# A graph layer on one core: 32 gathers taken from the input in the head, halved head products, constants written early, and columns fetched by ScalarE in two of five groups

## The chip, the core and the metric

The kernel runs on one core of a Trainium2 chip. A core has TensorE (PE in the profile, with its weight loads as PEld), VectorE (DVE), ScalarE (ACT), GpSimd (POOL) and SyncE (SP, which here only issues transfers); each works through its own instructions in their order. They share SBUF, 128 partitions of memory on the chip; matrix products end in PSUM, which DVE and ACT read. Transfers are done by 16 DMA engines, whichever engine issued them. The metric is the device time of one execution in microseconds.

## The reference

One message-passing layer over 12,500 nodes of 64 features and 412,500 edges, sorted by receiver, with 32 features each:

```python
h = jnp.maximum(_layernorm(x, axis=-1), 0.0)
msg_in = jnp.concatenate([h[src], h[dst], edge_attr_32], axis=-1)
messages = silu(msg_in @ W1 + b1) @ W2 + b2
att = jax.nn.softmax(silu(msg_in @ Wa1 + ba1) @ Wa2 + ba2, axis=0)   # over all edges
aggregated = jax.ops.segment_sum(messages * att, dst, num_segments=12500)
out = x + silu(jnp.concatenate([h, aggregated], -1) @ Wu1 + bu1) @ Wu2 + bu2
```

## The kernel before

**Tiling.** Nodes are padded to 98 blocks of 128 (NB = 98, NP = 12,544). Edges come in 403 groups (NG) of 1,024: K = 8 tiles of 128 edges. W1 and Wa1 stand side by side as 128 columns (C), so an edge has 128 sums before its activation: a sender's part, a receiver's part and an edge's part.

**Head** (`gnn_kernel`). Eight chunks of blocks (8, 14 five times, 12, 8) are loaded, normalized and turned (`squares`, `totals`, `deviation`, `normal`, `transpose`); the turned h stays in SBUF as `hT`, two nodes to a column of 128 rows. `senders` (L259-274) multiplies `hT` by the senders' half of the weights, one product of 128 rows by 256 columns for two blocks (L270), ACT copies the result out of PSUM (L272), and SP writes it as the table `ts_d`. Then `windows` computes each edge's offset from its group's first receiver, and the loop at L302-311 makes the receivers' table `tr_d` (L306 on PE, L308 on DVE, written from ACT's queue at L310). `hT_d` (L313) is a copy of `hT` that only `general` reads, the path for inputs that the main path can't take; it isn't run here.

**Main path** (`one_pass`). Constants, the loop's fixed buffers `acts` and `wins`, and the product W2 x Wu1 (`w2u`) are written at its start (L420-470). Per group g, in the order in which the engines get it:

- `begin(g)`: DVE adds what POOL gathered to the products (L573, and L575 for a column tile), ACT takes tanh (L576).
- pieces of `sum_up` for a group some five back: `out_of` copies its sums out of PSUM (L652, ACT), `put` adds them to the running sums (L671/L675/L678, DVE), `project` multiplies by `w2u` (L657), `by_node` makes the weights by receiver (L640, DVE) and sums over edges on PE (L646).
- `burst(g, 0)`: ACT fetches columns for a chosen group ahead, below.
- `load(g + 2)`: POOL gathers eight times 128 rows of `ts_d` by sender (L533) into one of the seven `gs` buffers of the pool `gather`; SP loads edges and receivers for four groups at a time (L544, L547) and two windows of `tr_d` (L554, three buffers); DVE makes the 0/1 matrix `eo` (L558); PE multiplies it with the window, which adds the receivers' and the edges' part (L562).
- `end(g)`: four DVE passes for message and logit (L586-L597), after every fourth group the maximum (`top`, with the exponentials in `weigh`, L627/L630 on ACT).
- `burst(g, 1)`: more columns.

POOL's gathers wait for nothing but the table, a free `gs` buffer and the eighth gather before. DVE, PE and ACT keep the written order (`pin`).

**Chosen groups.** In every third group from 8 to 390 (g % 3 = 1; 127 groups) the eighth tile isn't gathered. ACT copies, for each of its 128 edges, one column of `hT` (L504), whose number it first loads into a register (L500); a burst of 12 to 24 columns stands in each half of an iteration, six for a chosen group. `numbers` loads the sender indices, `places` computes column and parity on DVE (L487-L493, six operations), L567 zeroes the half that belongs to the other node, and PE multiplies by `stack` (L568), both halves of the senders' weights.

Of the kernel before, what the change touches and what calls it, by code (L numbers as in the profile page):

```python
# [53 lines left out]
P = 128  # L54
# [14 lines left out]
B = 4  # L69
NQ = 4  # L70
# [3 lines left out]
EVERY = 3  # L74
PHASE = 1
SLOTS = (((0, 24), (24, 24)), ((48, 24), (72, 12)), ((84, 24), (108, 20)))
# [7 lines left out]
PARTS = [("pair", 4 * C), ("we", C), ("bias", C), ("wu2h", 2 * D), ("wa2", U), ("bu2", D), ("w_bu", U),  # L84
         ("w2b", U), ("wu1a", U), ("wu2", D), ("ba2", 1), ("w_bup", 2 * U), ("bu1", 1)]
# [5 lines left out]
def gnn_kernel(ctx: ExitStack, tc: tile.TileContext, n_edges, x, src, src_row, dst, dst_row, first, edge,  # L91
# [14 lines left out]
    hT_d = dram.tile([2 * D, NB // 2, P], F32, name="hT_d")  # L106
# [19 lines left out]
    w_bu = part["w_bu"][:D + 1]  # L126
# [25 lines left out]
    nc.vector.memset(zero, 0.0)  # L152

# [8 lines left out]
    gather = ctx.enter_context(tc.tile_pool(name="gather", bufs=7))  # L162


    with tc.tile_pool(name="node1", bufs=1) as node1, \
            tc.tile_pool(name="node", bufs=2) as node, \
            tc.tile_pool(name="node_ps", bufs=2, space=PSUM) as node_ps:
        x_v = x.rearrange("(p b) d -> p b d", b=NB)

# [10 lines left out]
        nc.sync.dma_start(src_full, src)  # L180
# [11 lines left out]
        def windows():  # L192
# [6 lines left out]
            pin(nc.vector.tensor_tensor(dloc[:, T - K:], dloc[:, T - K:], real, ALU.mult))  # L199
            for h in range(2):  # L200
                pin(nc.vector.tensor_scalar(bj[:, :, h], base_full, iota_p, float(SHIFT * h),
                                            op0=ALU.add, op1=ALU.add))
# [13 lines left out]
        def subtract(i):  # L216
# [4 lines left out]
            xm = xms[i] = node.tile([P, CB, D], F32, name="xm", bufs=3)[:, :n, :]  # L221
# [36 lines left out]

        def senders(i, first, last):  # L259

            c, nn = chunks[i]
            last = min(last, nn)
            if first == 0:
                tss[i] = node.tile([P, CB, C], F32, name="ts")[:, :nn, :]
            ts = tss[i]
            for b in range(first, last, 4):
                m = min(4, last - b)
                pn = node_ps.tile([P, 4, C], F32, name="pn", bufs=4)
                for k in range(0, m, 2):
                    pin(nc.tensor.matmul(pn[:, k:k + 2, :], hT[:, (c + b + k) // 2, :],  # L270
                                         w_pair[:, 0], start=True, stop=True))
                pin(nc.scalar.copy(ts[:, b:b + m, :], pn[:, :m, :]))  # L272
            if last == nn:
                pin(nc.sync.dma_start(
                    ts_d.rearrange("(p b) f -> p b f", b=NB)[:, c:c + nn, :], tss.pop(i)))

# [5 lines left out]
        for i in range(nch + 1):  # L282
            if i < nch:
# [13 lines left out]
            if i < nch:  # L297
                normal(i)
        windows()
        for c, nn in chunks:  # L300
            tr = node.tile([P, CB, C], F32, name="tr")[:, :nn, :]
            for b in range(0, nn, 4):  # L302
                n = min(4, nn - b)
                pn = node_ps.tile([P, 4, C], F32, name="pn", bufs=4)
                for i in range(0, n, 2):
                    pin(nc.tensor.matmul(pn[:, i:i + 2, :], hT[:, (c + b + i) // 2, :],  # L306
                                         w_pair[:, 1], start=True, stop=True))
                pin(nc.vector.tensor_tensor(tr[:, b:b + n, :], pn[:, :n, :],  # L308
                                            bias[:, None, :].to_broadcast([P, n, C]), ALU.add))
            pin(nc.scalar.dma_start(  # L310
                tr_d[:NP, :].rearrange("(p b) f -> p b f", b=NB)[:, c:c + nn, :], tr))
        pin(nc.scalar.dma_start(tr_d[NP:, :], zero[:WR, :]))
        pin(nc.scalar.dma_start(hT_d, hT))  # L313
# [6 lines left out]


def node_bias(tc, b, v, work, ps):

    nc = tc.nc
    NB, w_bu = v["NB"], v["w_bu"]
    n = min(4, NB - b)
    hb = work.tile([D + 1, 4, P], F32, name="hb")
    nc.vector.memset(hb[D:, :, :], 1.0)
    for r in range(2):
        nc.sync.dma_start(hb[:D, r:n:2, :], v["hT_d"][r * D:(r + 1) * D, b // 2:(b + n) // 2, :])  # L330
    pb = ps.tile([P, 4, P], F32, name="mt")
    nc.tensor.matmul(pb[:U, :n, :], w_bu, hb[:, :n, :], start=True, stop=True)
    return pb[:U, :n, :]
# [60 lines left out]
def one_pass(tc, n_edges, v):  # L394
# [9 lines left out]
    ACTS, WINS, AHEAD = 8, 3, 2  # L404

    starts = list(range(0, NG - 11, B)) + [NG - 11, NG - 9] + list(range(NG - 7, NG))
    NS = len(starts)
# [4 lines left out]
    with ExitStack() as ctx:  # L412
# [6 lines left out]
        bases = keep.tile([33, NG + 1], I32, name="bases")  # L419
        base_lo, base_hi = bases[0:1], bases[32:33]  # L420
        nc.vector.memset(base_lo, 0)
        nc.vector.memset(base_hi, 0)
        nc.vector.tensor_scalar(base_lo[:, :NG], base_sb[:, :NG], float(NH), float(W),
                                op0=ALU.min, op1=ALU.add)
        nc.vector.tensor_scalar(base_hi[:, :NG], base_sb[:, :NG], float(W - NH), 0.0,
                                op0=ALU.add, op1=ALU.max)
        nmax = keep.tile([P, NS + 1], F32, name="nmax")
        nc.vector.memset(nmax[:, 0:1], BIG)
        scale = keep.tile([P, NS], F32, name="scale")
        total = keep.tile([P, 1], F32, name="total")  # L430
        nc.vector.memset(total, 0.0)
        start = keep.tile([P, 2], F32, name="start")
        nc.vector.memset(start[:, 0:1], 0.0)
        nc.vector.memset(start[:, 1:2], BIG)
# [706 lines left out]
```

## Time and profile before

| | us |
|---|---|
| median of 3 runs | 3992.78 (3986.42 to 3993.82) |
| the profiled execution, whole | 3986.92 |
| its span in the profile | 3985.1 |
| first gather starts | 49.82 |
| first group's addition (L573) starts | 94.58 |
| last gather ends | 3927.97 |

A line of the timeline reads: start, us, engine, line, operation, out<-in, count, and in brackets the engine's idle time ahead of it with what ended that. A line of groups gives the count, then busy us and mean ns of one, then the idle time ahead with its releasers. A line of waits gives us in total, times, and the longest. A line of stretches gives the length, then busy us with the number of instructions for PE, PEld, DVE, ACT and POOL, the granted TensorE clock, the DMA engines' busy share and GB/s. The mean granted clock of the execution was 0.64.

### The profile page before, as it was taken

The page shows a single profiled execution, that of the slowest core. Times are in us where ns is not written, and L with a number is a line of the kernel's source. Part 1 is how long each engine was busy: PE and PEld are TensorE (multiplying, and loading weights), DVE is VectorE, ACT ScalarE, POOL GpSimd, SP SyncE. Part 2 cuts the span into 40 slices and gives each one's busy share as a digit, 9 for nine tenths or more (in the row PEclk, how much of TensorE's full clock was granted, in tenths as well). Part 3 has the DMA queues.
Part 4 walks back from the last instruction along what each step waited for, and adds up shares of the span by engine and source line. Part 5 has one row for each costly group of instructions (what it writes and reads, how often), then busy time and mean ns, then how long its engine had stood idle before and what let it go on. Part 6 is the DMA issues. An engine that isn't in the chain of part 4 may idle for free. (4 is left out here: it accounts for less than half of the span.)

```text
span 3985.1 us, 80416 instructions
## 1 busy us (share of the span) xinstructions
PE 2332.9 (59%) x11238; PEld 1888.3 (47%) x11238; DVE 3264.8 (82%) x9553; ACT 2173.0 (55%) x17477; POOL 2950.2 (74%) x3122
## 2 busy tenths in 40 slices
PE   6556566666666555555555555555655555555566
PEld 5444444454444444444444444444544444444455
DVE  6888888888888787888878888887878887878787
ACT  3655555555555555555555555555555555555512
POOL 3777777777777777777777777777777777777774
PEclk8766666666666666666666666666666665666666
DMA  8333343333333333333333333333333333333333
GB/s 287 101 99 99 95 110 92 103 99 102 102 92 95 93 85 93 87 92 88 89 94 84 95 93 86 94 84 94 88 91 94 84 95 87 91 95 84 104 105 85
DMA packets 219778, 391.64 MB, mean 98 GB/s; under 512 B 72209, under 2 KB 146898, under 8 KB 206050
## 3 DMA queue, kind: packets, MB, share of 16 engines
q0 software_dynamic: 99104, 203.16, 19.1%
q1 hardware_dynamic: 118754, 173.60, 16.7%
q10 hardware_dynamic: 1376, 9.67, 0.6%
q14 instruction: 452, 3.70, 0.3%
q8 instruction: 92, 1.51, 0.2%
HBM read 360.42 MB, written 25.72 MB: 97 GB/s over the span
## 5 line engine op out<-in xcount | busy, mean ns | idle before, releaser
L533 POOL DMA_INDIRECT gs<-ts_d,src_sb x3097 | 2933.0, 947 | 992.6 <-issue 854.1
L562 PE MATMUL pe<-wins,eo 128*128 128x256 f32 x3224 | 1465.1, 630 | 925.7 <-DVE eo L558 679.6
L504 ACT COPY cols<-hT 128x1 f32 x16256 | 1605.0, 187 | 717.7 <-issue 714.8
L562 PEld LDWEIGHTS pe<-wins,eo 128*128 128x128 f32 x3224 | 970.9, 318 | 1222.7 <-DVE eo L558 769.0
L576 ACT ACTIVATE pe<-gs 128x1024 f32<-128x1024 f32 x403 | 413.7, 1026 | 928.6 <-DVE gs L573 496.8
L573 DVE TENSOR_TENSOR gs<-pe,gs 128x1024 f32<-128x1024 f32 (+1 forms) x403 | 475.4, 1180 | 393.6 <-DMA gs<-ts_d,src_sb 369.2
L640 DVE TENSOR_SCALAR wt<-iota_w,dloc,p 128x40 f32<-128x40 f32 x3224 | 726.1, 321 | 1.8
L646 PE MATMUL sp<-wt,acts 128*65 128x40 f32 x6448 | 628.8, 268 | 6.3 <-DVE wt L640 3.9
L646 PEld LDWEIGHTS sp<-wt,acts 128*65 128x65 f32 x6448 | 589.9, 183 | 16.2 <-DVE wt L640 9.7
L657 PEld LDWEIGHTS mt<-ss,w2u 65*128 65x128 f32 x806 | 203.0, 279 | 336.2 <-issue 173.9
L657 PE MATMUL mt<-ss,w2u 65*128 65x40 f32 x806 | 181.6, 319 | 242.3 <-DVE gm L623 202.0
L616 PE MATMUL mt<-ident,mx 128*128 128x128 f32 x107 | 47.4, 443 | 445.8 <-DVE sums L675 427.2
L594 DVE TENSOR_TENSOR pe<-pe,w_all 128x512 f32<-128x512 f32 x403 | 281.8, 699 | 13.4
L558 DVE TENSOR_SCALAR eo<-dbs,bj 64x256 f32<-64x256 int32 x806 | 277.9, 375 | 18.2 <-DMA dbs<-in_dst_row_dram 9.0
L592 DVE SCALAR_TENSOR_TENSOR pe<-pe,gs 128x512 f32<-128x512 f32 x403 | 280.3, 696 | 10.5
L586 DVE SCALAR_TENSOR_TENSOR acts<-pe,gs 128x512 f32<-128x512 f32 x403 | 277.2, 688 | 12.4 <-ACT pe L576 3.2
L597 DVE TENSOR_REDUCE lg<-pe 128x8 f32<-128x512 f32 x403 | 277.0, 687 | 10.5
L616 PEld LDWEIGHTS mt<-ident,mx 128*128 128x128 f32 x107 | 19.5, 182 | 456.9 <-issue 455.0
L678 DVE COPY stand<-nmax 64x40 f32 x806 | 161.0, 200 | 3.2
L671 DVE SCALAR_TENSOR_TENSOR sums<-sums,scale,mt 64x40 f32 x214 | 54.2, 253 | 89.2 <-PE mt L657 85.0
L675 DVE TENSOR_TENSOR sums<-sums,mt 64x40 f32 x592 | 111.5, 188 | 4.7 <-PE mt L657 0.6
L357 DVE TENSOR_SCALAR bu<-mt,w_all 64x256 f32<-64x256 f32 (+1 forms) x50 | 23.9, 477 | 88.7 <-PE mt L348 88.3
(124 smaller groups left out, 1062.7 us busy)
## 6 DMA issues: line engine op xcount, KB each, us to landing
eo<-in_edge_dram SPq DMA_DIRECT2D x100, 512.0 KB
dbs<-in_dst_row_dram SPq DMA_DIRECT2D x200, 256.0 KB
gs<-ts_d,src_sb POOLq DMA_INDIRECT x3097
wins<-tr_d SPq DMA_DIRECT2D x806, 32.0 KB
num<-in_src_row_dram SPq DMA_DIRECT2D x127, 64.0 KB
ts_d<-ts SPq DMA_DIRECT2D x5, 896.0 KB
tr_d<-tr ACTq DMA_DIRECT2D x5, 896.0 KB
hT_d<-hT ACTq DMA_DIRECT2D x1, 3136.0 KB
```

What stands on the lines that cost most here:

```text
L504: pin(nc.scalar.copy(to[:, first + i:first + i + 1], hT[:, bass.ds(regs[i], 1)]))
L533: nc.gpsimd.indirect_dma_start(out=full[:rows, j, :], out_offset=None, in_=ts_d[:, :], in_offset=bass.IndirectOffsetOnAxis(ap=src_full[:ro ...
L558: pin(nc.vector.tensor_scalar(eo[:WR, e], db[:, e], bj[g // NQ % 2 * WR:(g // NQ % 2 + 1) * WR, g, h:h + 1], None, op0=ALU.is_equal))
L562: pin(nc.tensor.matmul(pe[:, 2 * q:2 * q + 2, :], eo[:, q * EP:(q + 1) * EP], win[:, q // 2, :, :], start=True, stop=q < H - 1 or g not in ...
L573: pin(nc.vector.tensor_tensor(gss[g][:, :n, :], pes[g][:, :n, :], gss[g][:, :n, :], ALU.add))
L576: pin(nc.scalar.activation(pes[g], gss[g], AF.Tanh))
L586: pin(nc.vector.scalar_tensor_tensor(acts[g % ACTS][:, :, 0:U], th[:, :, U:C], 1.0, gs[:, :, U:C], op0=ALU.add, op1=ALU.mult))
L592: pin(nc.vector.scalar_tensor_tensor(att, th[:, :, 0:U], 1.0, gs[:, :, 0:U], op0=ALU.add, op1=ALU.mult))
L594: pin(nc.vector.tensor_tensor(att, att, wa2[:EP, None, :].to_broadcast([EP, K, U]), ALU.mult))
L640: pin(nc.vector.tensor_scalar(wt[:, j, :], iota_w[:EP, j // H, :], dloc[:, g * K + j:g * K + j + 1], p[:, k + j:k + j + 1], op0=ALU.is_equ ...
L646: pin(nc.tensor.matmul(sp, acts[g % ACTS][:, j, :], wt[:, j, :], start=j == 0, stop=j == K - 1))
L657: pin(nc.tensor.matmul(pp, w2u.rearrange("s h u -> s (h u)"), sps.pop(g), start=True, stop=True))
```

## The change

- **Raw groups.** For groups 0 to 3 (RAW = 4) POOL gathers 32 times 128 rows of x itself, at the start of the head, once a small load of their indices (first in SP's queue) has landed. The rows lie in two of the `gather` pool's buffers, two groups in each, and are normalized there edge by edge: DVE takes the sums of 64, ACT the squares with an accumulated sum (`raw_squares`, 16 activations for two groups) and a root, DVE the reciprocal and a product (`raw_scales`), ACT 16 Relu with scale and bias (`raw_normal`), PE turns them (`raw_turn`), ACT copies them back. The first two groups are done in the head: DVE's additions for `tr_d` stand behind their `raw_scales`. The second two groups' sums stand behind those additions; they are turned in iteration 0. `load(g)` for g < 4 multiplies them by the senders' weights into the same PSUM tile, with no gather from `ts_d`.
- **Halves.** Head products, senders' and receivers', are made as 64 rows by 128 columns (`rows_of`), the two halves into different PSUM banks; ACT and DVE take up to 8 blocks out of PSUM at a time instead of 4.
- **Early constants.** `acts` (6 instead of 8), `wins`, `stack`, `w2u` and the small constants are written at the start or in `products()`, which stands ahead of the second chunk in the head; the edge weights go into `wins` on ACT.
- **Columns.** g % 5 in (0, 3) from 10 to 390 are chosen, 153 groups; five bursts of 24 or 28 columns each, one in each half of an iteration. `column_lists` computes all columns and parities at once ahead of the loop and writes them to `list_d`; `listed` and `parity` load a group's row, 9 and 5 iterations ahead.
- **Buffers and moves.** `gs` has 6 buffers instead of 7; the sum goes into a separate tile `sm` (2 buffers), so a `gs` buffer is free after `begin(g)` instead of `end(g)`. `out_of`'s copy moves from ACT to DVE, behind the addition. `tr_d` is written from SP's queue. `hT_d` and `node_bias` are gone.

```diff
-EVERY = 3
-PHASE = 1
-SLOTS = (((0, 24), (24, 24)), ((48, 24), (72, 12)), ((84, 24), (108, 20)))
+EVERY = 5
+LEADS = {0: 9, 3: 10}
+SLOTS = ((0, 28), (28, 24), (52, 28), (80, 24), (104, 24))
+FIRST = 10
+RAW = 4
...
-    gather = ctx.enter_context(tc.tile_pool(name="gather", bufs=7))
+    gather = ctx.enter_context(tc.tile_pool(name="gather", bufs=6))
...
+        nc.sync.dma_start(src_full[:, :RAW * K], src[:, :RAW * K])
+        for g in range(RAW):
+            for j in range(K):
+                nc.gpsimd.indirect_dma_start(
+                    out=raws[g // 2][:, g % 2, j, :], out_offset=None, in_=x[:, :],
+                    in_offset=bass.IndirectOffsetOnAxis(ap=src_full[:, g * K + j:g * K + j + 1], axis=0))
...
+        def rows_of(pn, r, c, m):
+            for k in range(m // 2):
+                for h in range(2):
+                    rows = slice(h * D, (h + 1) * D)
+                    pin(nc.tensor.matmul(pn[:, h, k, :], hT[rows, c // 2 + k, :],
+                                         w_pair[rows, r, h * C:(h + 1) * C], start=True, stop=True))
...
+        def raw_squares(a):
+            flat = raws[a].rearrange("p r k d -> p (r k) d")
+            spare = node_ps.tile([P, 4, P], F32, name="pt")[:, 0, :D]
+            for i in range(RD):
+                pin(nc.scalar.activation(spare, flat[:, i, :], AF.Square, bias=raw_sum[a][:, i:i + 1],
+                                         accum_out=raw_sq[a][:, i:i + 1]))
+            pin(nc.scalar.activation(raw_dev[a], raw_sq[a], AF.Sqrt, bias=eps, scale=1.0 / D))
...
+        raw_means(0)
+        raw_squares(0)
         windows()
+        raw_scales(0)
+        raw_normal(0)
...
-            pin(nc.scalar.dma_start(
+            pin(nc.sync.dma_start(
                 tr_d[:NP, :].rearrange("(p b) f -> p b f", b=NB)[:, c:c + nn, :], tr))
-        pin(nc.scalar.dma_start(hT_d, hT))
+        for a in range(1, RAW // 2):
+            raw_means(a)
+            raw_squares(a)
...
+                    if g < RAW:
+                        turned = v["raws"][g // 2][:, g % 2].rearrange("p k d -> p (k d)")
+                        pin(nc.tensor.matmul(pe[:, 2 * q:2 * q + 2, :], turned[:, q * EP:(q + 1) * EP],
+                                             v["w_pair"][:, 0], start=False, stop=True))
...
-                pin(nc.vector.tensor_tensor(gss[g][:, :n, :], pes[g][:, :n, :], gss[g][:, :n, :], ALU.add))
+                sm = sms[g] = work2.tile([EP, K, C], F32, name="sm", bufs=2)
+                    pin(nc.vector.tensor_tensor(sm[:, :n, :], pes[g][:, :n, :], gs[:, :n, :], ALU.add))
...
-                pin(nc.scalar.copy(ss, sp))
+                pin(nc.vector.tensor_copy(ss, sp))
...
+            column_lists()
+            for a in range(1, RAW // 2):
+                v["raw_scales"](a)
+                v["raw_normal"](a)
             for g in range(AHEAD):
                 load(g)
```

292 lines of the change are left out of this document (167 added, 125 removed).

## The prediction

> **What bounds the kernel now.** I read the page's busy table first, then the costliest groups by form, the timeline at both ends of the gathers, the busy time by stretch, and last the waits.
>
> ```profile
> span 3985.1 us, 80416 instructions
> PE 2332.9 (59%) x11238; PEld 1888.3 (47%) x11238; DVE 3264.8 (82%) x9553; ACT 2173.0 (55%) x17477; POOL 2950.2 (74%) x3122
> L533 POOL DMA_INDIRECT gs<-ts_d,src_sb x3097 | 2933.0, 947 | 992.6 <-issue 854.1 <-DMA ts_d<-ts 47.4 <-DMA gs<-ts_d,src_sb 46.9
> 49.82 1.10 POOL L533 DMA_INDIRECT gs<-ts_d,src_sb  x1 [47.43 <-DMA ts_d<-ts]
> 51.23 0.94 POOL L533 DMA_INDIRECT gs<-ts_d,src_sb  x1 [0.30 <-issue]
> 3927.03 0.94 POOL L533 DMA_INDIRECT gs<-ts_d,src_sb  x1 [0.30 <-issue]
> 1000.00:2000.00 1000.00, 578.21 (x2833) 466.87 (x2832) 824.69 (x2439) 574.52 (x4771) 756.46 (x800) 0.64 0.35 92
> 2000.00:3000.00 1000.00, 578.39 (x2803) 471.30 (x2804) 815.23 (x2421) 569.25 (x4725) 756.47 (x800) 0.63 0.35 90
> DVE gs L573 <- DMA gs<-ts_d,src_sb: 369.2, 175, 6.5
> DVE acts L586 <- ACT pe L576: 3.2, 4, 1.8
> 3983.15 0.06 DVE hT L888
> ```
>
> The busy table misleads: DVE leads with 82%, POOL has 74%. But POOL's idle time is not slack. Of 992.6 us, 854.1 is "issue": the 0.30 us behind each gather (its own row says so), in which POOL waits for nothing. In both middle stretches (columns PE, PEld, DVE, ACT, POOL, each with its count) POOL starts exactly 800 gathers in 1000 us, one per 1.25 us. It runs without a real break from 49.82, where the last write of ts_d lands, to 3927.03 + 0.94 = 3927.97. So 3097 gathers take 3878.15 us, 1.2522 each with all hiccups. DVE, the busiest, waits for gathers 369.2 us and for ACT's tanh 3.2 us: it follows POOL. Time is therefore: start of the first gather of ts_d, plus their count times 1.2522, plus the 57.1 us from the last to the end of the span.
>
> **The change part by part: the count.** 403 groups have 8 gathers each; chosen groups drop one. Before, 127 are chosen: 3224 - 127 = 3097, the count in the row. Afterwards two residues of five from group 10 to 390 are chosen: 77 + 76 = 153. Groups 0 to 3 take none from ts_d; their 32 gathers read x and wait only for a small load of indices. Left are 399 x 8 - 153 = 3039, so 58 fewer: 26 because ACT fetches more columns, 32 because they run in the head, where POOL sits idle for 47.43 us. 32 x 1.2522 = 40.1 us from about 4 us on end near 44, ahead of ts_d. If a gather from x costs the 1.41 us that the first one took (49.82 to 51.23) they end at 49, if 0.94 at 34; nothing moves either way. 3039 x 1.2522 = 3805.5 us.
>
> **The start of the ts_d gathers.** ts_d is ready when the head's sender products are through.
>
> ```profile
> 30.00:40.00 10.00, 9.78 (x55) 8.25 (x54) 6.74 (x10) 8.97 (x21) 0.00 (x0) 1.00 0.67 260
> 20.00:30.00 10.00, 9.36 (x49) 7.85 (x49) 9.24 (x12) 8.38 (x19) 0.00 (x0) 1.00 0.51 200
> 38.28 0.85 PE L255 MATMUL pt<-ident,h 128*128 128x128 f32 x6
> 38.97 3.19 PE L270 MATMUL pn<-w_all,hT 128*128 128x256 f32 x14
> 45.23 1.07 ACT L272 COPY ts<-pn 128x512 f32<-128x512 f32 x2 [1.15 <-DMA ts_d<-ts]
> ```
>
> PE is 94 to 98% busy there, so its cost is on the path. A pass over 256 columns takes 3.19/14 = 0.228 us, and there are 98 for the senders: 22.3 us. In halves there are 196 passes over 128 columns. The nearest row is the transpose, 0.85/6 = 0.142 us: 27.8 us, so +5.5. From below: if two halves ran at once, 11 us would go, but DVE is 92% busy in the same stretch and ACT 90%, so no more than 8% of some 30 us comes through, -2.4. From above: each half as long as a whole pass, +22.3. I take +1.5, midway between the gain and the nearest row; products() (two small products, eight small ACT copies early) and the index load at the front of SP's queue lie inside it. 49.8 + 1.5 = 51.3.
>
> [...] No row here shows a 64-row product.
>
> **The start of the loop, and what its delay costs.** Here ACT and SP get new work, and the loop starts when the slowest is through.
>
> ```profile
> 47.40 3.53 DVE L308 TENSOR_TENSOR tr<-pn,w_all 128x512 f32<-128x512 f32 x6
> 68.93 1.29 DVE L308 TENSOR_TENSOR tr<-pn,w_all 128x512 f32<-128x512 f32 x2 [1.56 <-DMA tr_d<-tr]
> 73.52 0.40 DVE L421 MEMSET bases<- 1x404 int32 x1 [3.30 <-DMA tr_d<-tr]
> 90.79 8.16 PE L562 MATMUL pe<-wins,eo 128*128 128x256 f32 x24 [22.68 <-DMA wins<-tr_d]
> 94.58 1.23 DVE L573 TENSOR_TENSOR gs<-pe,gs 128x1024 f32<-128x1024 f32 x1 [4.44 <-PE pe L562]
> 117.15 1.23 DVE L573 TENSOR_TENSOR gs<-pe,gs 128x1024 f32<-128x1024 f32 x1 [0.21 <-issue]
> hT_d<-hT ACTq DMA_DIRECT2D x1, 3136.0 KB
> 95.87 1.28 ACT L576 ACT_TABLE_LOAD   x1 [49.57 <-DMA gs<-ts_d,src_sb]
> L630 ACT ACTIVATE p<-lg,nmax 128x32 f32<-128x32 f32 x98 | 30.0, 306 | 0.0
> L630 ACT ACTIVATION_READ_ACCUMULATOR p<-lg,nmax 128x1 f32 x107 | 20.0, 187 | 0.0
> ```
>
> ACT's 49.57 us wait in the head covers the normalization. A pair of groups takes 16 squares with an accumulated sum, at most 306 + 187 = 493 ns each by the last two rows, at least 306: 4.9 to 7.9 us, say 6.4; then a root, and 16 Relu at about 0.306: 4.9. For the first pair the squares run from ACT's last copy (45.23 + 1.07 + 1.5 = 47.8) to 54.2, and DVE's additions for tr_d stand behind the reciprocal that needs them: start about 55, not 47.40. They took 22.8 us with waits for landings, so end near 78; tr_d lands 3.3 later. The second pair's mean stands behind those additions on DVE, so its squares run 79 to 85.5, its Relu to 91. SP now queues the windows ahead of edges and receivers, without the wait for DVE's memsets and without 3.1 MB of hT_d in the way; windows, lists, edges, four issues more, land around 89. So the first group's addition begins at about 92 instead of 94.58. That the constants come early is worth nothing beside this: they were written inside the 22.68 us that PE waited.
>
> POOL has 6 buffers instead of 7, and two hold the raw rows. Four groups fill the free ones until 51.3 + 32 x 1.2522 = 91.4; group 8 needs the first raw buffer, free once group 1's products ran, just ahead of the first addition: 1 us lost. Group 10 is then due at 112.4 and needs group 4's addition done: the first five took 94.58 to 117.15, 22.6 us, so 92 + 22.6 + 1.2 = 115.8. Together 3.4 us. Each us that the loop starts later costs POOL one more; it has nothing queued but gathers, and DVE waits for them. Later groups ask for a buffer every 9.5 us, and DVE frees them faster (next).
>
> **The steady loop.** Five groups have 38 gathers: 47.6 us, 9.52 per group (before 23 in three, 9.60). Can the others keep that?
>
> ```profile
> L504 ACT COPY cols<-hT 128x1 f32 x16256 | 1605.0, 187 | 717.7 <-issue 714.8 <-DVE pe L592 2.9
> ACT cols L504 <- issue: 714.8, 1001, 1.7
> L576 ACT ACTIVATE pe<-gs 128x1024 f32<-128x1024 f32 x403 | 413.7, 1026 | 928.6 <-DVE gs L573 496.8 <-DVE gs L575 238.9 <-DMA gs<-ts_d,src_sb 187.9
> 2018.01 1.03 ACT L576 ACTIVATE pe<-gs 128x1024 f32<-128x1024 f32 x1 [2.06 <-DMA gs<-ts_d,src_sb]
> 2023.78 2.32 ACT L504 COPY cols<-hT 128x1 f32 x24 [1.46 <-issue]
> L627 ACT ACTIVATE scale<-fall 128x1 f32<-128x1 f32 x107 | 21.5, 201 | 60.4 <-DVE fall L626 59.9
> L652 ACT COPY ss<-sp 65x40 f32<-65x40 f32 x403 | 73.4, 182 | 13.0 <-PE sp L646 13.0
> L490 DVE TENSOR_SCALAR near<-near 1x128 f32<-1x128 f32 x127 | 37.4, 294 | 4.3
> L575 DVE COPY gs<-pe 128x128 f32<-128x128 f32 x127 | 35.5, 280 | 0.0
> SPq L554 <- PE pe L562: 1172.8, 173, 11.8
> ```
>
> ACT: a column costs 1605.0/16256 = 98.7 ns, a burst (six per chosen group, 762) 714.8/762 = 0.94 us of register loading ahead of it. Per five groups: 256 columns 25.3, ten bursts 9.4, five tanh 5.1, the exponentials (0.20 + 0.31 + 0.19, once in four groups) 0.9: 40.7 of 47.6 us. It fits. One group holds two bursts, 28 and 24 columns, behind its tanh. Before, a tanh at 2018.01 with 48 columns and the ss copy was through at 2026.10, 8.1 us; now 52 columns without the copy, about 8.3, under 9.52. The next tanh is ready when it is due, and DVE needs it only some 3 us later.
>
> DVE: the six index operations (near its largest, 0.294) go from 127 groups into 12 larger ones in the head, -0.5 us per group; the ss copy comes over from ACT, at most L575's 0.28, say 0.2; 26 more chosen groups add at most 0.05. DVE had 369.2/403 = 0.9 us per group to wait; it has some 1.1, less 0.08 of the shorter group. If the copy had no cover, it would be 403 x 0.2 = 81 us; the cover is this wait. PE gets 26 products and 32 passes, at 58% busy. SP gets 306 small list transfers for 127 loads of indices; it waits 1172.8 us for PE with the windows alone, so the 179 more issues cost nothing there.
>
> **Sum.** 51.3 + 3805.5 + 3.4 + 57.1 = 3917.3 us of span; the profiled execution took 3986.92 with a span of 3985.1, so 3919.1, which is 67.8 less. The runs' median, 3992.78, is 5.9 above that execution, their lowest, 3986.42, is with it; I add half of the 5.9: 3922.
>
> **Rivals.** (a) The head gives much back. If a 64-row pass is as long as a whole one, ts_d comes 22.3 later and tr_d's products, on the same terms, hold the loop some 44 us longer, 136 instead of 92: POOL, out of buffers at 112, stands until 136. 3922 + 21 + 23 = 3966. For it: PE is the bound of the head. Against: the transposes' 0.142 us. (b) The gathers from x do not fit into the head, because they share the transfers with loads of x and wait for the eighth before them; then nothing of the 40 us is won: 3962. Against: transfers took half to two thirds of their time from 20 to 40 us (0.51 and 0.67 in the rows). (c) Slower: ACT becomes the bound of the loop. Mean register loading of 0.94 us per burst leaves room; it decides from (47.6 - 25.3 - 5.1 - 0.9)/10 = 1.63 us. With every burst at the longest, 1.7, and the exponentials' waits for DVE between them (60 us in 107 batches, 0.7 per five groups) five groups take 49.0: 106 us more over 380 groups, 4028. Break-even is 68 x 5/380 = 0.9 us beyond 47.6, 1.72 per burst without those waits. For it: gaps of 1.46 and 1.7 exist, ahead of second bursts, and bursts are longer now. Against: they are tails, the mean is 0.94. (d) Better: halves side by side and no buffer wait, 3922 - 3.9 - 3.4 = 3915.
>
> **Numbers.** Forecast 0.70, with a range of its own from 3908 to 3938; (a), whole or half, 0.12; (b) 0.05; (c) 0.08; (d) 0.05. The range takes in the forecast, (d), (b) from the lower side and half of (a): 3904 to 3958. A measurement here tells 0.2%, 8 us, from no change. Everything but (c) is faster by more: faster 0.91; same 0.02, (c) at its break-even; slower 0.07.
>
> **What would show it.** POOL's count of 3039 from ts_d at 1.25 us each, from about 51 to 3860, and 32 from x done by 45; one or two POOL waits for DVE or PE between 91 and 116; first addition near 92; ACT's issue time ahead of columns near 720 us in all. I would be wrong if DVE or ACT waited for the other in the middle stretches, so that POOL started fewer than 800 gathers per 1000 us.

## The result, and the profile after

The changed kernel takes 3963.06 us (median of 4 runs, 3961.32 to 3969.41), before 3993.18 beside it: ratio 0.9929, 95% interval 0.9913 to 0.9945, some 28 us less (0.0071 x 3993). The forecast was 3922 in a range from 3904 to 3958: the sign was right, the size wrong by 41 us. Here are the lines of the profile after, to be held against those before: first the page's head, and from the groups by line the gathers from ts_d, those from x, and the columns,

```profile
span 3961.3 us, 86004 instructions
PE 2343.1 (59%) x11534; PEld 1926.1 (49%) x11534; DVE 3154.9 (80%) x9242; ACT 2442.2 (62%) x20499; POOL 2927.3 (74%) x3096
L599 POOL DMA_INDIRECT gs<-ts_d,src_sb x3039 | 2875.7, 946 | 973.5 <-issue 827.1 <-DMA gs<-ts_d,src_sb 57.3 <-DVE wt L714 24.1
L203 POOL DMA_INDIRECT gs<-in_x_dram,src_sb x32 | 34.4, 1074 | 10.1 <-issue 9.4 <-DMA src_sb<-in_src_dram 0.6
L569 ACT COPY cols<-hT 128x1 f32 x19584 | 1919.0, 187 | 892.9 <-issue 811.6 <-PE sp L720 45.8 <-PE mt L731 18.5
```

then busy time by stretch (PE, PEld, DVE, ACT, POOL),

```profile
30.00:40.00 10.00, 5.63 (x58) 4.79 (x58) 6.44 (x9) 6.89 (x13) 7.72 (x8) 0.86 0.66 235
1000.00:2000.00 1000.00, 603.10 (x2935) 495.91 (x2936) 822.13 (x2440) 659.04 (x5739) 750.30 (x795) 0.63 0.37 94
2000.00:3000.00 1000.00, 586.45 (x2863) 484.76 (x2861) 793.30 (x2353) 640.73 (x5576) 756.17 (x801) 0.63 0.35 91
```

and the timeline of POOL, with DVE's last addition and last instruction:

```profile
45.90 0.94 POOL L203 DMA_INDIRECT gs<-in_x_dram,src_sb  x1 [0.31 <-issue]
56.18 0.94 POOL L599 DMA_INDIRECT gs<-ts_d,src_sb  x1 [9.34 <-DMA ts_d<-ts]
94.86 0.95 POOL L599 DMA_INDIRECT gs<-ts_d,src_sb  x1 [0.30 <-issue]
111.87 0.94 POOL L599 DMA_INDIRECT gs<-ts_d,src_sb  x1 [16.06 <-issue]
3895.11 0.94 POOL L599 DMA_INDIRECT gs<-ts_d,src_sb  x1 [0.30 <-issue]
3902.67 1.23 DVE L647 TENSOR_TENSOR sm<-pe,gs 128x1024 f32<-128x1024 f32 x1
3953.90 0.06 DVE L969 MEMSET hT<- 128x1 f32 x1
```

The count is as forecast: 3039 gathers from ts_d and 32 from x, the last of which ends at 46.84. But POOL stands still for 16.06 us at 94.86, and it starts 795 gathers in the second thousand us, the sign that the forecast had named against itself. Against the forecast's sum (own span each; the stalls are POOL's gaps beyond the usual 0.31 us, added up over its whole timeline):

| term | forecast | measured | difference |
|---|---|---|---|
| start of the first gather from ts_d | 51.3 | 56.2 | +4.9 |
| 3039 gathers without stalls | 3805.5 | 3801.8 | -3.7 |
| wait for a buffer at the loop's start | 3.4 | 16.4 | +13.0 |
| stalls later on, all between 500 and 1280 us | 0 | 21.7 | +21.7 |
| last gather to the end of the span | 57.1 | 65.2 | +8.1 |
| span | 3917.3 | 3961.3 | +44.0 |

**The late loop.** The timeline of ACT, SP, DVE and PE between the last addition for tr_d and the first group of the loop:

```profile
92.76 0.31 ACT L353 ACTIVATE raw_dev<-raw_sq,eps 128x16 f32<-128x16 f32 x1
93.10 0.50 SPq L610 DMA_DIRECT2D eo<-in_edge_dram  x1
93.64 0.58 SPq L613 DMA_DIRECT2D dbs<-in_dst_row_dram  x1
101.97 1.14 DVE L624 TENSOR_SCALAR eo<-dbs,bj 64x256 f32<-64x256 int32 x4 [8.41 <-DMA dbs<-in_dst_row_dram]
102.52 1.19 PE L628 MATMUL pe<-wins,eo 128*128 128x256 f32 x2 [23.16 <-DMA eo<-in_edge_dram]
107.72 1.22 DVE L645 COPY sm<-pe 128x1024 f32<-128x1024 f32 x1 [4.61 <-PE pe L633]
```

The first load of edges (L610) goes out at 93.10, right after ACT's root (L353, 92.76 + 0.31) has read eps for the last time. eps lies in the head's pool node1, and the edges' buffers come into that memory. DVE's wait for the receivers, whose load goes out at 93.64, ends 8.3 us later, and the first group gets to DVE at 107.72; the forecast had 92. POOL is through its free buffers at 95.8 and waits.

**The tile stage.** From group 16 to about 120 the loop also prepares the biases of the output tiles (tile_bias, twice in eight groups). DVE's waits between 500 and 1200 us (total, times, longest):

```profile
DVE bu L448 <- PE mt L439: 73.0, 18, 4.5
DVE sums L745 <- PE mt L731: 30.3, 16, 2.3
...
DVE sm L647 <- DMA gs<-ts_d,src_sb: 1.3, 7, 0.2
```

One of them in the timeline of PE and DVE:

```profile
912.04 3.75 PE L628 MATMUL pe<-wins,eo 128*128 128x256 f32 x8 [1.55 <-issue]
915.59 1.06 PE L439 MATMUL mt<-hT,w_all 128*128 128x256 f32 x2
916.69 0.98 DVE L448 TENSOR_SCALAR bu<-mt,w_all 64x256 f32<-64x256 f32 x2 [4.48 <-PE mt L439]
```

In these 700 us DVE waits for gathers 1.3 us in all: it is the bound. It stands 4.48 us for a product (L439) that PE gets to only behind the next group's eight passes (L628, 3.75 us). Before, the same wait was there between 500 and 1200 us and did no harm, although DVE waited for gathers only 1.8 us in all there too:

```profile
DVE bu L357 <- PE mt L348: 62.3, 18, 4.5
DVE gs L573 <- DMA gs<-ts_d,src_sb: 1.8, 9, 0.2
```

What differs is DVE's pace and the room that it has behind POOL when it enters this stage; the run without raw rows, below, measures both.

Three theories were set against each other: H, the late loop start; T, the tile stage, where DVE is slower than POOL; and C, the denser columns, which hold ACT and through it DVE.

### The profile page after: what moved, and what is told of

Read it like the earlier page. It is cut to its first block, busy times and chain, and to the rows that moved or that the text cites. A ratio compares the mean times of both kernels' runs of the same rounds, so it can differ in the third digit from the quotient of the medians.

```text
span 3961.3 us, 86004 instructions
## 1 busy us (share of the span) xinstructions
PE 2343.1 (59%) x11534; PEld 1926.1 (49%) x11534; DVE 3154.9 (80%) x9242; ACT 2442.2 (62%) x20499; POOL 2927.3 (74%) x3096
## 5 line engine op out<-in xcount | busy, mean ns | idle before, releaser
L599 POOL DMA_INDIRECT gs<-ts_d,src_sb x3039 | 2875.7, 946 | 973.5 <-issue 827.1
L569 ACT COPY cols<-hT 128x1 f32 x19584 | 1919.0, 187 | 892.9 <-issue 811.6
L628 PE MATMUL pe<-wins,eo 128*128 128x256 f32 x3224 | 1470.6, 635 | 1016.8 <-issue 643.7
L628 PEld LDWEIGHTS pe<-wins,eo 128*128 128x128 f32 x3224 | 997.5, 325 | 1289.6 <-issue 732.2
L650 ACT ACTIVATE pe<-sm 128x1024 f32<-128x1024 f32 x403 | 411.0, 1020 | 506.8 <-DVE sm L647 232.2
L647 DVE TENSOR_TENSOR sm<-pe,gs 128x1024 f32<-128x1024 f32 (+1 forms) x399 | 466.6, 1170 | 244.6 <-DMA gs<-ts_d,src_sb 226.9
L720 PE MATMUL sp<-wt,acts 128*65 128x40 f32 x6448 | 620.4, 268 | 4.8 <-DVE wt L714 4.0
L720 PEld LDWEIGHTS sp<-wt,acts 128*65 128x65 f32 x6448 | 585.3, 183 | 10.7 <-DVE wt L714 6.6
L660 DVE SCALAR_TENSOR_TENSOR acts<-pe,sm 128x512 f32<-128x512 f32 x403 | 278.0, 690 | 60.1 <-ACT pe L650 51.1
L666 DVE SCALAR_TENSOR_TENSOR pe<-pe,sm 128x512 f32<-128x512 f32 x403 | 281.6, 699 | 13.1
L624 DVE TENSOR_SCALAR eo<-dbs,bj 64x256 f32<-64x256 int32 x806 | 266.4, 368 | 16.2 <-DMA dbs<-in_dst_row_dram 8.4
```

Of the source, the lines that this page charges most:

```text
L569: pin(nc.scalar.copy(cols[g][:, first + i:first + i + 1], hT[:, bass.ds(regs[i], 1)]))
L599: nc.gpsimd.indirect_dma_start(out=full[:rows, j, :], out_offset=None, in_=ts_d[:, :], in_offset=bass.IndirectOffsetOnAxis(ap=src_full[:ro ...
L628: pin(nc.tensor.matmul(pe[:, 2 * q:2 * q + 2, :], eo[:, q * EP:(q + 1) * EP], win[:, q // 2, :, :], start=True, stop=g >= RAW and (q < H - ...
L647: pin(nc.vector.tensor_tensor(sm[:, :n, :], pes[g][:, :n, :], gs[:, :n, :], ALU.add))
L650: pin(nc.scalar.activation(pes[g], sm, AF.Tanh))
L660: pin(nc.vector.scalar_tensor_tensor(acts[g % ACTS][:, :, 0:U], th[:, :, U:C], 1.0, gs[:, :, U:C], op0=ALU.add, op1=ALU.mult))
```

## The experiments

Ratios are to the kernel before, run on the same chip with each set of runs; the median of before differed from set to set (3987.5 to 3993.8 us), so versions are compared by their ratios, one thousandth being 4 us. The intervals are some 0.0017 to either side. Times inside the head are those of one profiled execution each. In eleven executions whose head is the same up to there, the first gather from ts_d started between 52.24 and 54.79, in a twelfth, the changed kernel's own above, at 56.18; differences of 1 to 3 us there show little by themselves.

**The changed kernel again, as the measure for the rest.**

> The changed kernel once more, unchanged, beside the next three on one chip and with the same runs of before: ratio 0.993, that is some 30 us less than before; stall at the loop's start 15 to 18 us, stalls between 400 and 1300 us together 20 to 25 us. All theories expect the same.

Ratio 0.9933 (0.9917 to 0.9950). First gather from ts_d 52.97, first addition 106.12, stall 17.7 us, later stalls 20 us. So 3 us of the first gather's 4.9 belong to that one execution. Its granted clock was 0.83, 0.86 and 0.80 in the ten us from 20, 30 and 40; the repeat's was 1.00 in all three (the row from 30 to 40 below, 0.86 in the row above). That the clock made the 3 us is likely and not shown. When the first gather starts earlier the stall only gets longer, since the loop's start sets its end.

```profile
30.00:40.00 10.00, 7.11 (x98) 6.26 (x98) 8.01 (x12) 8.81 (x16) 7.87 (x8) 1.00 0.75 272
```

**Head, first edit.**

```
-        eps = node1.tile([P, 1], F32, name="eps")
+        eps = const.tile([P, 1], F32, name="eps")
```

> The constant eps stands in memory of its own, so that the first loads of edges need not wait until the second pair's root has read it. Theory H (the loop starts late because these loads come into memory that the root, done at 93.07, still reads): the first edge load is issued near 88, not 93.10, the first group's addition comes at about 98 instead of 107.72, POOL's stall of 16.06 us shrinks to 6 to 8, and the time falls by 8 to 10 us to about 3954. Rival O (SP's order behind the list writes, or the windows, holds them): first addition 105 or later, stall over 13 us, time within 3 us of 3963.

Its timeline (SP, DVE, POOL):

```profile
83.35 0.52 SPq L610 DMA_DIRECT2D eo<-in_edge_dram  x1
99.53 1.23 DVE L645 COPY sm<-pe 128x1024 f32<-128x1024 f32 x1 [6.14 <-PE pe L633]
103.69 0.94 POOL L599 DMA_INDIRECT gs<-ts_d,src_sb  x1 [11.56 <-issue]
```

Ratio 0.9917. The load goes out 9.8 us earlier than in the changed kernel, though the additions for tr_d began only 3.7 earlier; the first addition comes 6.6 us before that of the repeat, the stall is 6.1 shorter. The mechanism is shown, its price is two thirds of what H expected. The later stalls stay, 23 us.

**Tile stage.** tile_bias becomes a generator: its product is issued ahead of the next group's products (the first `next`), its additions at their old place (the second).

```
+                biased = None
+                if g >= 16 and g // 8 - 2 < NT and g % 8 in (1, 5):
+                    biased = tile_bias(tc, (g // 8 - 2) * NC, g % 8 == 1, v, work2, one_ps, bus)
+                    next(biased, None)
                 if g + AHEAD < NG:
                     load(g + AHEAD)
...
-                if g >= 16 and g // 8 - 2 < NT and g % 8 in (1, 5):
-                    tile_bias(tc, (g // 8 - 2) * NC, g % 8 == 1, v, work2, one_ps, bus)
+                if biased:
+                    next(biased, None)
```

> The product of the tile stage is queued on PE ahead of the next group's products, its two additions on DVE stay behind them. Theory T (from group 16 to about 120 DVE is the bound, because it waits 101.8 us in 25 waits of up to 4.5 us for this product): that wait falls under 40 us, POOL's stalls of together 27 us between 500 and 1280 us go, time about 3963 - 27 = 3936. Rival C (the denser columns on ACT hold DVE back, through the tanh and through PE): the stalls stay above 18 us in all, time 3955 or more.

DVE's wait in the whole span, the changed kernel first, then this one:

```profile
DVE bu L448 <- PE mt L439: 101.8, 25, 4.5
```

```profile
DVE bu L449 <- PE mt L439: 9.2, 19, 0.7
```

Ratio 0.9875 (0.9859 to 0.9891), 23 us less than the changed kernel; no stall is left after 140 us. These are T's figures; rival C's did not come.

**Head, second edit.** The first pair's reciprocal and Relu move behind two chunks of additions for tr_d, the second pair's means and squares up to the fifth chunk.

```
         windows()
-        raw_scales(0)
-        raw_normal(0)
         for c, nn in chunks:
+            if c == chunks[min(2, nch - 1)][0]:
+                raw_scales(0)
+                raw_normal(0)
             if c == chunks[min(4, nch - 1)][0]:
                 raw_turn(0, node_ps, "pt")
+                for a in range(1, RAW // 2):
+                    raw_means(a)
+                    raw_squares(a)
...
-        for a in range(1, RAW // 2):
-            raw_means(a)
-            raw_squares(a)
```

> In the head the first pair's reciprocal, product and Relu stand behind the first two chunks of additions for tr_d, and the second pair's mean and squares ahead of the fifth chunk. Theory H: additions from about 55.5 instead of 61.05, tr_d written some 5 us earlier, second pair's squares over by about 82, so the first addition of the loop comes at 92 to 95 instead of 107.72 and POOL's stall falls from 16.06 to 1 to 4; time 3963 - 13 = about 3950. Rival O: the additions wait for tr_d's landings and for PE instead, the first addition comes after 103, time within 5 us of 3963.

```profile
51.61 3.21 DVE L414 TENSOR_TENSOR tr<-pn,w_all 128x1024 f32<-128x1024 f32 x3
95.07 1.22 DVE L646 COPY sm<-pe 128x1024 f32<-128x1024 f32 x1 [7.09 <-PE pe L634]
99.22 0.94 POOL L600 DMA_INDIRECT gs<-ts_d,src_sb  x1 [7.20 <-issue]
```

Ratio 0.9903, 12 us less, as H expected; first addition at 95.07. The stall is 7.20 and not 1 to 4, because in this execution POOL's gathers too began earlier, at 52.24. The later stalls stay, 19 us.

**No raw rows.** RAW = 0 and no calls of the raw_ functions: all groups gather from ts_d.

> No raw rows: all groups gather from ts_d, the denser columns and everything else stay, so 3224 - 153 = 3071 gathers. Theory H with T (a late loop start leaves DVE almost six groups behind, and that is why its slow tile stage stalls POOL): without the normalization the loop starts near 88, POOL has 32 gathers more before it, DVE enters the tile stage close behind POOL and no stall over 3 us appears: 54 + 3071 x 1.2522 + 57 + 2 = about 3958 to 3964, the 32 gathers from x then being worth next to nothing as the change stands. Rival C: POOL's stalls between 500 and 1280 stay near 27 us and the time is 3980 or more.

Ratio 0.9928: the 32 gathers from x, forecast at 40 us, are worth nothing in the changed kernel. The first gather starts at 51.88, not one stall follows, and 3071 gathers take 1.2504 us each. To see why, the pace of both engines was worked out from the timelines, from the starts of each group's gathers and of its addition. The room is the time from the end of the addition that frees a buffer to the gather that uses it next, the smallest of twenty groups:

```
                     us per group, groups 20-99    room, groups   smallest room,
                     DVE     POOL                  20-39          groups 20-139
before (7 buffers)   9.64    9.62                  45.9           43.1
changed              9.90    9.71                   5.3            0.3
no raw rows          9.93    9.52                  30.2            2.3
old columns          9.76    9.62                  13.8            3.3
ss on ACT            9.47    9.52                  16.4           15.6
product first        9.22    9.52                  14.3           14.3
```

In the kernel before, a buffer is free only behind the four DVE passes; to the last of them that read it, its room is 41.2 and 36.8. DVE has the same 9.9 us per group with and without raw rows, against POOL's 9.52. Without them it enters the stage with 30 us of room and leaves it with 2.3. With them POOL has run out of buffers at the loop's start; however short that stall is, it leaves DVE six buffers behind, so the stage begins with next to no room and each hiccup of DVE stops POOL. That is why the head's edits alone (0.9917 and 0.9903) shorten the first stall and leave the later ones. The paces in the last two rows are no limits: there DVE catches up with POOL or follows it.

**All three edits.**

> The three edits together: eps in memory of its own, the normalization spread among the additions for tr_d, the tile stage's product ahead of the group's products on PE. Theory H with T: the two gains add, since the one lies before 130 us and the other between 400 and 1300: 10 to 11 from the head and 21 to 24 from the tile stage, so 31 to 35 us less than the changed kernel; one stall of about 7 us at the loop's start is left. Rival: with DVE ahead of time the next stage becomes the bound (PE's or ACT's part of the loop), new stalls appear and under 25 us are won.

Ratio 0.9852, 32 us less; one stall of 6.6 us. The gains add.

**ss back on ACT.**

```
-                pin(nc.vector.tensor_copy(ss, sp))
+                pin(nc.scalar.copy(ss, sp))
```

> The copy ss goes back from DVE to ACT, all else as in the changed kernel. Theory T (DVE is the bound from group 16 to about 120): 0.18 us and its wait for PE leave DVE in each of some 92 groups, 0.2 to 0.3 us apiece, so the stalls between 400 and 1300 us fall from 22 to under 5 and the time by 15 to 20 us. Rival A (in that stage it is ACT, busy with columns, that DVE waits for): the copy comes late out of ACT, the waits for it on PE and DVE grow, and the time is the same within 5 us or longer.

Ratio 0.9866, 27 us less than the repeat of the changed kernel, more than T expected: the later stalls are gone, though the tile stage's wait stays (79.8 us between 400 and 1300). DVE's pace falls from 9.90 to 9.47, more than the copy's own 0.186 us: the waits for ACT's tanh and for PE's sums shrink with it (10.7 to 0.7 and 42.7 to 35.5 us there). The tail is 3 us shorter as well (62.6). Rival A is out: ACT has the time.

**The old columns.** The dense columns serve two of five groups, the old ones one of three.

```
-EVERY = 5
-LEADS = {0: 9, 3: 10}
-SLOTS = ((0, 28), (28, 24), (52, 28), (80, 24), (104, 24))
+EVERY = 3
+LEADS = {1: 10}
+SLOTS = ((0, 24), (24, 24), (48, 24), (72, 12), (84, 24), (108, 20))
```

> The columns as before in one of three groups (six bursts of 24, 24, 24, 12, 24, 20), the raw rows and everything else as changed: 3224 - 32 - 127 = 3065 gathers from ts_d, 26 more. Theory T: DVE's rate in the tile stage stays, only POOL asks 0.08 us per group less, so stalls of about 15 of the 22 us stay and the time is 3959 + 26 x 1.25 - 7 = 25 us above the changed kernel, near before. Rival C (the denser columns made DVE late): the stalls between 400 and 1300 us vanish, and the time is only 10 us above the changed kernel.

Ratio 0.9961, 11 us more than the changed kernel, with no later stall: the number that C gave, and T's missed. By the table both act: POOL asks 0.1 us per group later, and DVE is 0.14 us per group faster, so the denser columns do cost DVE time in the tile stage. C alone does not hold: with the same dense columns two other edits end the stalls.

**Whole passes in the head.** rows_of issues one product of 128 rows by 256 columns for two of 64 by 128.

> The head's products again as whole passes of 128 rows by 256 columns, everything else as changed. In the changed kernel 16 passes of 64 rows by 128 columns took 1.16 us (0.073 each), so a pair of halves costs 0.146 where a whole pass cost 0.228: 98 x 0.082 = 8 us of PE for the senders and as much for the receivers. Theory P (PE is still on the head's path): the first gather from ts_d moves from 53 to 56 to about 61 to 64, the loop starts 8 to 16 us later and the time rises by 8 to 16 us. Theory A (ACT's copies and the landings of ts_d and tr_d set the head's pace now): both move by less than 3 us and so does the time.

Ratio 0.9945 (0.9928 to 0.9961), not to be told from the changed kernel. First gather 55.40 and first addition 108.61, each 2.4 to 2.5 later than in the repeat: nearer to theory A. Against the eleven executions with halves (52.24 to 54.79) the first gather is 0.6 to 3.2 later, so the halves win a little ahead of ts_d, and how much stays open. The first addition tells nothing: it came between 103.74 and 110.00 in executions whose head is the same to its end.

**Three edits and ss on ACT.**

> The three edits of the run before last (eps, normalization spread, tile stage's product first) and ss on ACT. Theory T: with no stall left in the tile stage the copy's return wins nothing there, only in the tail, where DVE then begins the last group some 3 us after its gathers instead of 6 to 7: about 3 us less than with the three edits, 3925. Rival: the copy on ACT delays the products behind it, and the time is 3930 or more.

3925.04 us (3923.65 to 3927.27), ratio 0.9840 (0.9824 to 0.9856), and no stall but the first, of 8.1 us. That is 3 to 5 us less than without ss on ACT, inside the intervals; the span does show a tail 3.9 us shorter (65.7 to 61.8). It is faster than before and than the changed kernel, the latter by 37 us (0.0093 x 3988). Below it is called the best version.

**The end of the span.** Three memsets of one column are left out; they only wait for outputs.

> Left out are the three memsets of one column behind the end, which compute nothing and only wait for the outputs to land. Before they stood behind the branch over the general path, in the changed kernel ahead of it. Theory E (the branch, 5.4 us in all, now comes after the landings instead of beside them): the span ends 2 to 4 us after the last output is issued and landed instead of 9.1 us after its issue, the time falls by 4 to 6 us to about 3955. Rival: the end is set by something else, change under 1 us.

Ratio 0.9923, no measurable gain, and the span still ends 9.2 us after SP has issued the last output (3948.47 to 3957.7; 9.1 in the changed kernel, 4.9 before). Theory E falls. The trace shows what holds the end: POOL's closing instruction, a drain, which the page doesn't count as busy. The view of the kernel's closing line gives count, least, median and greatest ns, and first and last start; the changed kernel first, then before:

```profile
L1224 POOLq DRAIN  x3: 40/107/8477, 3952.0 to 3961.0; - x3
L1137 POOLq DRAIN  x3: 40/107/1943, 3978.0 to 3984.8; - x3
```

In the changed kernel the long drain runs from 3951.98 to 3960.45, while SP and DVE are through by 3955.2; before, it ends at 3979.93, ahead of SP and DVE. It takes 8.48 us in every version with the dense columns, this one too, and 1.94 in the three with columns in one of three groups.

**All together.** Beside the edits above, products() behind the senders (called after windows(), ahead of the raw rows' scales) and no memsets.

> All together: the three edits, ss on ACT, products() moved from the head's start to behind the senders' products, and the three memsets left out. Theory: the gains of head, tile stage, tail and end add, 3925 - 5 for the end, and 2 to 4 us for the head, where ACT is free of 3.5 us of small copies ahead of the first hT copy, so that ts_d and tr_d come earlier: 3916 to 3918. Rival: products() behind the senders delays the raw rows on ACT by the same 3.5 us, and the head gives nothing: 3920.

A miss: 3930.86, ratio 0.9856, 6 us slower than the best version beside it. The first gather comes earlier (50.95), but the loop's first addition 1.7 us later (98.96 against 97.25), and the stall is 12.5 us instead of 8.1. ACT's small copies had only moved into the loop's way, and an earlier first gather is lost in the stall.

**What the raw rows are worth when nothing else stalls.** No raw rows, eps in memory of its own, the product first, ss on ACT.

> No raw rows, with the tile stage's product first and ss on ACT: nothing should stall, 3071 gathers from about 52. Theory (a gather taken off POOL's run is worth 1.25 us once no stall eats it): last gather at 52 + 3071 x 1.2504 = 3892, tail 62 to 63, so a span near 3955 and a time near 3956, 31 us above the version with raw rows and all edits (3925): the head's normalization takes 9 of the 40. Rival: the raw rows win less than 20 us even so.

Ratio 0.9923 against 0.9840: 33 us, by the two spans 29 (3954.5 and 3925.6), where 31 were expected. 3071 gathers without a stall, 1.2504 each.

**products() among the additions for tr_d**, ahead of the seventh chunk, in the best version.

> The version with the three edits and ss on ACT (3925), and products() behind the second pair's squares, among the additions for tr_d, where ACT waits 7 us. Theory: first gather near 51 as in the run before, and the loop's first addition 2 to 3 us earlier than 97.25 too, since nothing of the raw rows is held; stall 7 to 8, time 3922 to 3923. Rival: the first addition does not move, the stall is 11, the time the same within 1 us.

Ratio 0.9845 (0.9829 to 0.9862), the same. First gather 50.85, so ACT's small copies had cost 2.8 us of it, but first addition 96.19, only 1.1 earlier, and a stall of 9.8: between theory and rival, and no gain in time.

**What the columns are worth when nothing else stalls.** The best version with the old columns.

> The version with the three edits and ss on ACT (3925), but the columns in one of three groups: 26 more gathers from ts_d. Theory: with no stall in the tile stage in either, 26 x 1.25 = 32.5 us more, 3957. Rival: ACT's denser columns cost something elsewhere in the loop, and the difference is under 25.

Ratio 0.9934, 37 us more, where 32.5 were expected: by the timelines the first stall is 3.5 us longer and a gather takes 1.2530 us instead of 1.2510 (why, is open; the last run below has 1.2525 with dense columns, so it is not the columns alone), 6 us in all, and the end is shorter. DVE's last line here, in a span of 3963.1, then that of the version with dense columns, in a span of 3925.6:

```profile
3960.93 0.06 DVE L975 MEMSET hT<- 128x1 f32 x1
```

```profile
3917.66 0.06 DVE L975 MEMSET hT<- 128x1 f32 x1
```

With old columns the span ends 2.1 us after the last memset, with dense ones 7.9. So it is in the run with old columns before this one (2.0), in before (1.9), and in the changed kernel (7.3): the extra 5.4 us at the end come with the denser columns, by POOL's drain, which takes 1.94 us here and 8.48 there. Why it takes longer stays open. POOL issues 3097 gathers in each of the three kernels with old columns and 3071 in each of the others, so that the columns themselves and POOL's count are not told apart.

**The path that isn't executed, made shorter.** general loses the part that prepares its biases; it is not executed on these inputs.

> The changed kernel without the part of the general path that prepares its biases (general is not executed on these inputs). Theory L (the length or place of the code that the closing branch jumps over sets the end): the span ends 3 to 5 us after the last output has landed instead of 7.5, the time falls by up to 5 us. Rival: no change, the 7.5 us stay.

Ratio 0.9914, 6.9 us from the last memset to the end: no change, and POOL's drain takes the same 8.48 us. Theory L falls too.

## Why the prediction was right in its count and wrong in its size

- **The count and the cadence were right.** 58 gathers fewer, 1.25 us each: where nothing stalls behind the loop's start, the 32 are worth 29 to 33 us, net of the head's work, and the 26 are worth 37 (the runs without raw rows and with old columns, beside the best version). The 1.2522 that I took, "with all hiccups", was even 0.0012 too long, 3.7 us of the sum.
- **The first gather from ts_d: 51.3 forecast, 52.2 to 56.2 in the kernels with raw rows and products() early, 50.9 with products() moved.** The term "products() ... lie inside it" was too small: ACT copies 3.5 us ahead of the first hT copy, and some 2.8 of them come through (50.85 against 53.66 in the best version). It cost nothing in time, as the loop's start came later still.
- **The halves came out better than forecast**: +1.5 was taken, a gain of 0.6 to 3.2 us was measured, around the lower bound of -2.4. Sixteen passes take 1.16 us (row below), 0.073 each, so a pair takes 0.146 against 0.228 whole, both at a granted clock of 1.00, and about as long as one transpose (0.95/7 = 0.136, second row). From 30 to 40 us PE spent 7.8 us on 35 whole passes before and 3.3 us on 44 halves in the changed kernel, at a granted clock of 0.86; in the repeat the 98 passes of that stretch, 84 halves among them, took 7.11 us. (The changed kernel's 5.63 busy us of ten, beside 9.78 before, hold less work, those 44 halves.) What makes a pair shorter than a whole pass is not shown.

```profile
30.26 1.16 PE L305 MATMUL pn<-w_all,hT 64*128 64x128 f32 x16 [0.51 <-ACT hT L298]
32.41 0.95 PE L296 MATMUL pt<-ident,h 128*128 128x128 f32 x7 [0.98 <-DVE h L284]
```

- **The failed step: "the first group's addition begins at about 92 instead of 94.58".** I let windows, lists and edges land around 89 and asked for each queue's order, but not whose memory the edges' buffers take. They wait for the last reader of a one-column constant; with the constant elsewhere, the load went out at 83.35 instead of 93.10. The additions for tr_d also came 6 us later than forecast (61.05 for 55, behind the last senders' copy at 51.85 and the squares) and so did all that follows them. The term of 3.4 us for POOL's wait was 16.4. It was too small by its own working, too: the 1 us lost ahead of group 8 and the 3.4 from 112.4 to 115.8 make 4.4. The rule that I gave for it, each us of delay costs POOL one more, held within 2.2 us: the loop came 15.7 later, POOL's first gather 4.9, and the stall grew by 13. The first raw buffer also came free later than I had it, not just ahead of the first addition, but 4.15 us after its start (107.72 to 111.87, behind group 1's products).
- **The second failed step: "later groups ask for a buffer every 9.5 us, and DVE frees them faster".** With it the sum had no stalls later on; they were 21.7 us. It was taken from DVE's mean slack, 369.2 us over 403 groups, and that slack isn't spread evenly: between 500 and 1200 us DVE had 1.8 us of it, as the trace of before already showed (row above). Between groups 16 and 120 DVE now needs 9.9 us per group and has none; before, some 41 us of room and a pace of 9.64 hid that. The copy ss, of which I wrote "the cover is this wait", had no cover there: off DVE, 27 us come back. That the busy table misleads, as I wrote at the start, holds of a wait summed over the span just as well.
- **The tail** was taken over as 57.1 and is 65.2. Four of the 8.1 us are DVE's lateness: the last group's addition begins 6.6 us after the gathers' end (3896.05 to 3902.67), before 2.6; with the three edits and ss on ACT it is 2.8 (3863.72 to 3866.50). 5.4 are POOL's longer closing drain, less 1.4 between.
- **Rivals.** (b) did not come: the gathers from x fit with 9 us to spare. (c), ACT as the bound, did not come either, with 811.6 us of issue time (forecast near 720) over 765 bursts, 1.06 each, where 1.63 decides; a weaker form did, ACT's columns slowing DVE by 0.14 us per group. (a) had the place nearly right, POOL out of buffers while the loop starts late, and nearly the time, 3966, but by the wrong cause, so that the nearness is luck: a 64-row pass took 0.073 us and not 0.228, and with whole passes the first gather comes no more than 3.2 us later.

## What to carry to other kernels

A mean slack covers a new cost only if it is there in every stage (DVE's was 369.2 us before, 1.8 of it between 500 and 1200 us): take the window in which the engine waits least, and see what it waits for there. When a pool's memory was used again here, the first load into it waited for the last reader of a small constant that lay there (93.10 us, and 83.35 with the constant elsewhere); a constant that is read late belongs elsewhere. Room between producer and consumer is a stock: what a late start uses up is missing in the slow stage 400 us later (5.3 us of room at its start, against 30.2 without raw rows). A wait at the end is looked for on every engine, also among instructions that the page doesn't count as busy (here a drain of 8.48 us).

## What the runs showed of the hardware

- In the changed kernel PE starts the loop's first passes at 102.52, after 23.16 us without work. The granted clock was 0.50 from 81.6 to 105.45 and 1.00 from 105.55 to 122.5: pairs of passes of 256 columns took 1.19 and twice 1.06 us in the first of these stretches, and 0.59 each in the second. From start to start the first four pairs took 3.27 us (102.52 to 105.79), the next four 1.72 (105.79 to 107.51), so the first group paid some 1.5 us, by the author's estimate from these times.

```profile
104.36 1.06 PE L628 MATMUL pe<-wins,eo 128*128 128x256 f32 x2
...
106.65 0.59 PE L628 MATMUL pe<-wins,eo 128*128 128x256 f32 x2
```

- Gathers from x move rows of half the length, and take POOL the same 0.94 us (the last at 45.90) as those from ts_d; the mean of 1.07 comes from eleven that took 1.04 to 1.68 us, the last of them at 31.75.
- POOL's drain at the end of the program takes 8.48 us in all kernels with 3071 gathers and 1.94 in the three with 3097, and holds the end in the former, 5.3 us after SP and DVE are through in the changed kernel (3955.2 to 3960.45). Neither leaving out the closing memsets nor a shorter path not taken changes it.
